# Transposing the later sequences on VectorE in 32x32 squares, with DMA moving the squares, in a linear-attention and FFN kernel

## The chip, the cores and the metric

The kernel runs on one core of a Trainium2 chip. It is one launch, all in fp32, and the time is that of the device in microseconds (us), the median of several runs. The names used below: PE is the matrix engine (TensorE), PEld its weight load, DVE is VectorE, ACT is ScalarE, POOL is GpSimd, and SP is the engine whose queue issues nearly all DMA transfers.

## The reference

The input is x, 8 sequences of 512 tokens with 512 features. The reference, cut to what matters:

```python
xn = layernorm(x)                                   # over the features
q, k, v = (xn @ W.T + b for W, b in ...)
phi = lambda t: elu(t) + 1
ctx = phi(q) * cumsum(phi(k) * v, axis=tokens) * 32 ** -0.5
s = ctx @ Wo.T + bo                                 # linear attention
h = fwht(xn * SU_ug)                                # Walsh-Hadamard transform
h = silu((h @ W_gate.T) * scale_g) * ((h @ W_up.T) * scale_u)
f = (fwht(h * SU_dp) @ W_down.T) * scale_d          # hidden size 2048
out = x + s * silu(f)
```

The matrix products want the features of xn on the partitions, so each normalized sequence has to be transposed, from tokens x features to features x tokens, before anything else can be done with it.

## The kernel before

**Passes.** The 8 sequences are handled in four passes (p = 0 to 3) of two sequences each. The two sequences of a pass are put side by side as one 1024-token operand, and each product with a weight matrix is done by a seven-product scheme in the manner of Strassen and Winograd: the operand and the weights are cut into 2x2 blocks and encoded by additions and subtractions into seven factors, and seven products P1, P2, P7, P3, P4, P5, P6 take the place of eight. The gate and up products of passes 1 to 3 apply the scheme twice, an outer and an inner one. The Hadamard transforms are folded into the weights during pass 0.

**The token operand xo.** `xo` holds the encoded tokens: seven outer factors, and for each of them seven inner factors. Of the outer ones, P1 and P2 come from the even sequence of a pair and P7 and P3 from the odd one; P5, P6, P7 and P4 are then subtractions of these. The function `transposed` (L165 to L183) makes them: for each 128 tokens of a sequence, PE transposes four 128x128 squares into a PSUM bank of tag "t" (L170), ACT copies them into `xo` (L174 for the even sequence, L177 for the odd one), and DVE makes the differences straight from PSUM (L178 to L180), and P4 at the end (L183). `inner_tokens` (L185 to L189) makes the inner P5, P6 and P4 with three subtractions of 128x1792, and `inner_t3` the inner P7 later.

**One pass.** The main loop (L986 to L1033) does, for each pass: attention (`attention`), then four hidden units u = 0 to 3 (gate, up, silu and product; `gate` and `up` in pass 0, `hidden_unit` in passes 1 to 3), with the output projection of the attention (`project_out`) inside u = 0. The product with W_down is done in halves: `down(p, 0)` after u = 1, whose result is stored to DRAM (`put_by`), and `down(p, 1)` after u = 3, which adds the first half back in, applies silu, multiplies with s and adds x. At u = 3 (pass 0) or u = 2 (passes 1 and 2), `next_x` loads the next two sequences and normalizes them (`load_x`, `layernorm`); `transposed` for both comes right before `down(p, 1)`, and then the first half d, the attention's s and the residual y are fetched.

**Products of the down projection.** `token_groups` (L404 to L501) does the seven products for two row groups g = 0, 1, each in its own PSUM bank of tag "px" (three banks) and "pz" (two banks), while tag "py" has one bank for both. The order is P1 and P7 of both groups, then P2 of g 0, P6 of g 0, P2 of g 1, P6 of g 1, and then P5, P3 and P4 of both groups. `read` (L425 to L432) takes a px bank into sa, sb or sc with an addition of the first half (L431), and `output` (L434 to L437) adds py or pz to that (L435). In the very last `down`, P4 of group 1 is done in two chunks of 128 rows, each with its own addition (L480) and its own end of the work (`gated_last`, L765 to L770).

**What sets the order.** A product is not issued where it is written, but put on an agenda by `at(place, ...)`, where a place is about one product later than the one before; `advance` works the agenda off. Work inside `background()` gets a lower priority. The planner of the framework then fixes the order of the instructions on each engine when the kernel is built, by priorities and its own estimates, so the order on each engine is the same in every run. Weights come through a queue three deep (`ask(3)`) into a pool of four tiles. The pools that matter here: `xin` has one tile (the sequence just loaded), `t8` six tiles of 1 MB, `snap` six, `xop` one.

Of the kernel before, what the change touches and what calls it, by code (L numbers as in the profile page):

```python
# [21 lines left out]
def kernel(  # L22
# [27 lines left out]
    nc = tc.nc  # L50
# [54 lines left out]
    def load_x(b, t=None, parts=1):  # L105
        if t is None:
            t = xin.tile([P, 3, 7, P], F32, tag="x", name=f"x_{b}")
            t = t.rearrange("p c s e -> p (c s e)")[:, : NT * D].rearrange("p (n d) -> p n d", n=NT)
        n = NT // parts
        for i in range(0, NT, n):  # L110
            nc.sync.dma_start(
                t[:, i : i + n], x[b, i * P : (i + n) * P, :].rearrange("(n p) d -> p n d", p=P)
            )
        return t
# [19 lines left out]
    def first_layernorms(xs):  # L134


        mv = small.tile([P, 2 * NT, 2], F32, tag="mv2", bufs=1, name="mv_first")
        rs = small.tile([P, 2 * NT, 2], F32, tag="rs2", bufs=1, name="rs_first")
        then = []

        def pinned(ins):
            tc.keep_in_program_order(ins)

        for i in range(2 * NT + 1):
            if i < 2 * NT:
                x, r = xs[i // NT][:, i % NT, :], rs[:, i, 0:1]
                st = small.tile([P, 6], F32, tag="st2", bufs=4, name=f"st_first_{i}")
                pinned(nc.vector.bn_stats(st, x))
                pinned(nc.vector.bn_aggr(mv[:, i, :], st))
                pinned(nc.vector.tensor_scalar(r, mv[:, i, 1:2], EPS, None, ALU.add))  # L150
                nc.scalar.activation(r, r, AF.Sqrt)
            if i:
                x, m, r = xs[(i - 1) // NT][:, (i - 1) % NT, :], mv[:, i - 1, 0:1], rs[:, i - 1, 0:1]
                n = rs[:, i - 1, 1:2]
                pinned(nc.vector.reciprocal(r, r))
                if i <= NT:
                    pinned(nc.vector.scalar_tensor_tensor(n, m, -1.0, r, ALU.mult, ALU.mult))
                    nc.scalar.activation(x, x, AF.Identity, bias=n, scale=r)
                else:
                    pinned(nc.vector.tensor_scalar(x, x, m, r, ALU.subtract, ALU.mult))  # L160

# [164 lines left out]
        advance(max([0] + [e[0] + 1 - now[0] for e in agenda]))  # L328

    def bank(tag, name, n):  # L330
        return ps.tile([P, n, L // n], F32, tag=tag, bufs={"px": 3, "py": 1, "pz": 2}[tag], name=f"{tag}_{name}")


    def group(name, ws, rhs, dst, then, bias=(None, None)):
# [69 lines left out]
    def token_groups(name, n, tok, wts, dst, add=None, early=None, done=None, last=None):  # L404

        px, py, pz = {}, {}, {}
        sums, ws = {}, {}

        def product(p, i, g, first, ks=None, cs=range(2)):
            if i not in ws:
                ws[i] = wts(i)
            for k in ks or range(n):
                t = tok(k, i)
                for c in cs:
                    nc.tensor.matmul(  # L420
                        p[:, c], t[:, (2 * g + c) * P : (2 * g + c + 1) * P], ws[i](k),
                        start=(first and k == 0 and c == 0), stop=(k == n - 1), skip_group_check=True,
                    )

        def read(what, o, a, s, g):  # L425
            if o is None:
                o = snap.tile([P, 2, 2 * P], F32, tag="s", name=f"{what}_{name}_{g}")
            if add is None:
                nc.scalar.copy(o, px[g])
            else:  # L430
                nc.vector.tensor_tensor(o, px[g], add(a, s, g), ALU.add)  # L431
            return o  # L432

        def output(o, p, a, s, g):  # L434
            nc.vector.tensor_tensor(dst(a, s, g), o, p, ALU.add)  # L435
            if done:
                done(a, s, g)  # L437

        def p1(g, ks=None):
            if g not in px:  # L440
                px[g] = bank("px", f"{name}_{g}", 2)
            product(px[g], P1, g, True, ks)
            if ks is None or n - 1 in ks:
                sums["a", g] = read("sa", None, 0, 0, g)

        def p7(g, ks=None):
            if g not in pz:
                pz[g] = bank("pz", f"{name}_{g}", 2)
            product(pz[g], P7, g, True, ks)

        def p2(g):
            py[g] = bank("py", f"{name}_{g}", 2)
            product(py[g], P2, g, True)
            output(sums["a", g], py[g], 0, 0, g)

        def p6(g):
            product(px[g], P6, g, False)
            sums["b", g] = read("sb", None, 1, 0, g)

        def p5(g):  # L460
            product(px[g], P5, g, False)
            s = read("sc", None, 1, 1, g)
            output(s, pz[g], 1, 1, g)

        def p3(g):
            product(px[g], P3, g, False)
            read("", dst(0, 1, g), 0, 1, g)
            if done:
                done(0, 1, g)

        def p4(g):
            if g == 0 or not last:
                product(pz[g], P4, g, False)
                output(sums["b", g], pz[g], 1, 0, g)
                return
            for c in range(2):
                product(pz[g], P4, g, False, cs=(c,))
                s = slice(c, c + 1)
                o = dst(1, 0, g)[:, s]
                nc.vector.tensor_tensor(o, sums["b", g][:, s], pz[g][:, s], ALU.add)  # L480
                last(c)

        steps = [(p, g) for p in (p1, p7) for g in range(2)]
        place = 0
        if early:
            a, b = range(early), range(early, n)
            for p, g in steps:
                at(place, lambda p=p, g=g: p(g, a))
                place += early
            place = max([place] + [e[0] - now[0] for e in agenda])  # L490
            for p, g in steps:
                at(place, lambda p=p, g=g: p(g, b))
                place += n - early
            steps = []
        steps += [(p2, 0), (p6, 0), (p2, 1), (p6, 1)]
        steps += [(p, g) for p in (p5, p3, p4) for g in range(2)]
        for p, g in steps:
            at(place, lambda p=p, g=g: p(g))
            place += n
        advance(place)  # L500
        between()  # L501
# [127 lines left out]
    def fetch(name):  # L629
        t = t8.tile([P, NT, D], F32, tag="t", name=name)  # L630
        nc.sync.dma_start(t.rearrange("p n d -> p (n d)"), kept[name])
        return t
# [353 lines left out]
    for p in range(B // 2):  # L986
        if p:
            with background():
                inner_tokens(xo)
        co = attention(p, xo, get_w)  # L990
        if p:
            inner_t3(xo, (P1, P5, P6, P2, P7))
            at(9, lambda: inner_t3(xo, (P3, P4)))
        more = p + 1 < B // 2
        hos = []

        def next_x():
            xs = [load_x(2 * p + 2), load_x(2 * p + 3)]
            for s in range(2):
                layernorm(2 * p + 2 + s, xs[s])  # L1000
            return xs

        for u in range(NU):
            if p == 0:
                gs = [gate(p, u, xo, get_w)]
                gs.append(gate(p, u + NU, xo, get_w))
                if u == 0:
                    project_out(p, co, get_w)
                ho = hop.tile([P, 2, 7, L], F32, tag="h", name=f"ho_{p}_{u}")
                for m in range(2):  # L1010
                    up(p, u + m * NU, gs[m], xo, ho[:, m], get_w)
            else:
                ho = hop.tile([P, 2, 7, L], F32, tag="h", name=f"ho_{p}_{u}")
                hidden_unit(p, u, xo, ho, get_w, u % 2 == 1)
                if u == 0:
                    project_out(p, co, get_w)
            hos.append(ho)
            if more and u == (2 if p else 3):
                xs = next_x()
            if u == 1:  # L1020
                down(p, 0, hos, get_w)
                hos = []
        if more:
            xo = xop.tile([P, 7, 7, H], F32, tag="xo", name=f"xo_{p + 1}")
            for s in range(2):
                transposed(2 * p + 2 + s, xs[s], xo)
        ds, ss = [], []
        for s in range(2):
            ds.append(fetch(f"d_{p}_{s}"))
            ss.append(fetch(f"s_{p}_{s}"))  # L1030
        ys = [load_y(p, s) for s in range(2)]
        down(p, 1, hos, get_w, ds, ss, ys)
        drain()  # L1033

# [49 lines left out]
```

## Time and profile before

| | |
|---|---|
| median of 3 runs | 1601.99 us (1600.81 to 1603.28) |
| profiled execution | 1604.14 us |
| its span, first to last instruction | 1602.3 us |
| mean granted PE clock | 0.991 of full speed |
| PE busy | 1553.3 us (97%) |
| DVE busy | 944.5 us (59%) |
| ACT busy | 429.0 us (27%) |
| POOL busy | 505.7 us (32%) |
| DMA | 254.29 MB in 148,043 packets, 7,296 of them under 512 bytes |

How to read it: busy time is the time in which an engine had an instruction in work, as a share of the span. The profile also has a chain of work that ended last, followed back from the last instruction, which says on which engine the time lay; groups of instructions by line, engine and shape, with their number, busy time, mean duration and the idle time before them with what ended it; a list of what each engine waited for ("PE px_dn L420 <- DVE sb_dn L431: 1.7, 2, 0.9" says that PE at L420 waited for the DVE instruction of L431 1.7 us in all, 2 times, 0.9 at most); a timeline of single instructions; and windows, which give the busy time of each engine in a stretch of time and the clock that PE was granted in it.

### The profile page before, as it was taken

What the parts mean: (1) busy time and instruction counts of PE and PEld (TensorE: products, weight loads), DVE (VectorE), ACT (ScalarE), POOL (GpSimd) and SP (SyncE); (2) the same over time, 40 slices, a digit from 0 to 9 for tenths busy, and PEclk for the clock granted to TensorE, in tenths of its full rate; (3) what the DMA queues carried; (4) which work ended last, traced back from release to release, by engine and by line L of the source; (5) the groups of instructions that cost most, each with busy time, mean ns of one, the idle gap of its engine ahead of it and who ended that gap; (6) DMA issues with size and microseconds to landing.
All of it is one profiled execution on the core that took longest, in us unless ns stands there. A gap on an engine that the chain in (4) does not pass through costs nothing.

```text
span 1602.3 us, 15711 instructions
## 1 busy us (share of the span) xinstructions
PE 1553.3 (97%) x5936; PEld 1118.1 (70%) x5936; DVE 944.5 (59%) x1346; ACT 429.0 (27%) x688; POOL 505.7 (32%) x286
## 2 busy tenths in 40 slices
PE   7889889999999999999999999999999999999998
PEld 3336435854485488888886478888887468888887
DVE  6868666268564574715675475634675466542673
ACT  4342332132324431111223531111221441111211
POOL 4531342104331335302622236201622137120731
PEclk9999989999999999999999999999999999999999
DMA  8234559287753244335564232535574224425472
GB/s 273 81 118 122 180 156 298 79 280 223 254 214 121 71 137 152 124 116 189 177 247 145 92 111 100 190 91 188 161 263 157 69 92 138 174 86 190 141 257 88
DMA packets 148043, 254.29 MB, mean 159 GB/s; under 512 B 7296, under 2 KB 109696, under 8 KB 143872
## 3 DMA queue, kind: packets, MB, share of 16 engines
q1 hardware_dynamic: 147824, 253.26, 47.9%
q8 instruction: 47, 0.77, 0.2%
q14 instruction: 28, 0.23, 0.0%
q10 hardware_dynamic: 144, 0.03, 0.0%
HBM read 183.53 MB, written 69.73 MB: 158 GB/s over the span
## 4 chain that ended last, share of the span: by engine, by line
PE 78%; DVE 9%; DMA 4%; POOL 3%; issue 3%; ACT 2%; SPq 0%; POOLq 0%; ACTq 0%; DVEq 0%
PE px_gu L512 18%; PE pz_gu L512 9%; PE px_dn L420 8%; PE py_gu L512 5%; PE pz_dn L420 4%; PE px_o L420 3%; PE px_v L344 3%; PE px_k L344 3%; PE px_q L344 3%; PE px_gate L344 2%; PE px_up L344 2%; PE py_dn L420 2%; POOL s L757 2%; PE pz_o L420 2%; PE pz_k L344 2%
## 5 line engine op out<-in xcount | busy, mean ns | idle before, releaser
L512 PE MATMUL px_gu<-xo,w_gu 128*128 128x256 f32 x1344 | 320.6, 379 | 0.0
L512 PEld LDWEIGHTS px_gu<-xo,w_gu 128*128 128x128 f32 x1344 | 254.6, 190 | 40.0 <-issue 3.6
L420 PE MATMUL px_dn<-w_down,ho 128*128 128x256 f32 x1024 | 230.1, 379 | 2.4 <-DVE sb_dn L431 1.7
L420 PEld LDWEIGHTS px_dn<-w_down,ho 128*128 128x128 f32 x1024 | 193.6, 190 | 31.7 <-DVE sb_dn L431 2.7
L512 PE MATMUL pz_gu<-xo,w_gu 128*128 128x256 f32 x672 | 173.1, 380 | 0.0
L712 POOL TENSOR_TENSOR u<-u,v 128x1024 f32<-128x1024 f32 x24 | 56.1, 2362 | 354.2 <-DVE u L550 354.2
L512 PEld LDWEIGHTS pz_gu<-xo,w_gu 128*128 128x128 f32 x672 | 127.0, 190 | 19.2 <-DVE a L554 0.9
L420 PE MATMUL pz_dn<-w_down,ho 128*128 128x256 f32 x512 | 116.9, 380 | 3.7 <-POOL ho L200 1.9
L420 PEld LDWEIGHTS pz_dn<-w_down,ho 128*128 128x128 f32 x512 | 96.3, 190 | 19.7 <-POOL ho L200 2.7
L757 POOL TENSOR_TENSOR s<-s,d 128x512 f32<-128x512 f32 x30 | 43.1, 1437 | 166.1 <-ACT d L756 166.1
L512 PE MATMUL py_gu<-xo,w_gu 128*128 128x256 f32 x336 | 86.2, 379 | 0.0
L600 POOL TENSOR_TENSOR v<-v,k 128x1024 f32<-128x1024 f32 x16 | 39.4, 2463 | 138.0 <-ACT v L575 109.8
L674 POOL TENSOR_TENSOR ho<-g,u 128x512 f32<-128x512 f32 x8 | 17.8, 2226 | 187.1 <-DVE u L360 187.1
L512 PEld LDWEIGHTS py_gu<-xo,w_gu 128*128 128x128 f32 x336 | 63.8, 190 | 8.7
L344 PE MATMUL px_k<-xo,w_k 128*128 128x512 f32 x128 | 63.1, 615 | 3.5 <-ACT sa_k L356 3.5
L344 PE MATMUL px_up<-xo,w_up 128*128 128x512 f32 x128 | 61.5, 609 | 3.5 <-DVE w_up L206 3.5
L716 POOL TENSOR_TENSOR v<-v,r 128x1024 f32<-128x1024 f32 x24 | 56.2, 2360 | 25.6 <-DVE r L550 25.6
L344 PE MATMUL px_v<-xo,w_v 128*128 128x512 f32 x128 | 60.4, 593 | 2.0 <-ACT sc_v L356 2.0
L344 PE MATMUL px_q<-xo,w_q 128*128 128x512 f32 x128 | 60.2, 593 | 0.0
L602 DVE TENSOR_TENSOR_SCAN k<-ones,v 128x512 f32<-128x512 f32 x32 | 39.4, 1271 | 34.9 <-POOL v L600 34.9
L344 PE MATMUL px_gate<-xo,w_gate 128*128 128x512 f32 x128 | 59.6, 593 | 0.0
L420 PE MATMUL px_o<-w_o,co 128*128 128x256 f32 x256 | 58.3, 381 | 0.0
(254 smaller groups left out, 2472.1 us busy)
## 6 DMA issues: line engine op xcount, KB each, us to landing
w_gu<-d_gu SPq DMA_DIRECT2D x84, 896.0 KB, 4.5
w_down<-d_down SPq DMA_DIRECT2D x56, 512.0 KB, 3.6
d_s<-o SPq DMA_DIRECT2D x8, 1024.0 KB, 4.9
d_d<-dn SPq DMA_DIRECT2D x8, 1024.0 KB, 7.4
d<-d_d SPq DMA_DIRECT2D x8, 1024.0 KB, 6.2
s<-d_s SPq DMA_DIRECT2D x8, 1024.0 KB, 7.4
y<-in_x_dram SPq DMA_DIRECT2D x8, 1024.0 KB, 7.8
out_dram<-y SPq DMA_DIRECT2D x15, 512.0 KB, 3.1
```

The source lines that it names most:

```text
L344: nc.tensor.matmul(p.rearrange("p a t -> p (a t)") if len(r.shape) == 2 else p, ws[k][:, i, :], r, start=(first and k == 0), stop=(k == n ...
L420: nc.tensor.matmul(p[:, c], t[:, (2 * g + c) * P : (2 * g + c + 1) * P], ws[i](k), start=(first and k == 0 and c == 0), stop=(k == n - 1), ...
L512: nc.tensor.matmul(p[:, lane], w[:, lane, i, :], x[:, i, :], start=(first and lane == 0), stop=True, skip_group_check=True,)
L600: nc.gpsimd.tensor_tensor(v[:, h], v[:, h], k[:, h], ALU.mult)
L602: nc.vector.tensor_tensor_scan(k[:, h, s], ones.to_broadcast([P, L]), v[:, h, s], 0.0, ALU.mult, ALU.add)
L674: nc.gpsimd.tensor_tensor(ho[:, P1], g[:, 0, 0], r[:, 0, 0], ALU.mult)
L712: nc.gpsimd.tensor_tensor(r[:, m], ru1[:, m], rv[:, m], ALU.add)
L716: nc.gpsimd.tensor_tensor(rv[:, m], rv[:, m], rr[:, m], ALU.add)
L757: (nc.vector if final and (a, s) == (1, 0) else nc.gpsimd).tensor_tensor(r, r, d, ALU.mult)
```

## The change

The first two sequences are transposed by PE as before. For the other six:

- `normalized(b)` loads and normalizes one sequence and stores it back to a DRAM buffer of its own. It is called, with background priority, in the hidden units u = 0 and u = 1 of each pass but the last, one sequence in each; `next_x` is gone.
- `squares(b)` loads it again, in four DMA transfers, such that each run of 32 features of one token goes to the partition that the transposed layout wants for this token's place in its group of 32. One transfer fills 32 partitions with 64 x 32 elements each, in runs of 128 bytes. The tile z that it fills is the `xin` tile for an even sequence and a `t8` tile for an odd one.
- `turned` transposes the 32x32 squares in place with `nc.vector.transpose` on DVE, one instruction for 128 partitions x 512 elements, four for a sequence, straight from z into `xo`.
- `next_tokens` takes the place of the two calls of `transposed`: loads, the transposes, and the four outer differences as subtractions of 128x1024. The second half of the odd sequence with two of the differences is put on the agenda at place 5, and P4 at place 10.
- `xo` is no longer allocated anew in each pass: the same tile is written again.
- d is fetched for both sequences at once, s at place 7 of the agenda and y at place 15.
- In the last `down`, P7 and P4 of group 1 use two banks, one for each chunk of rows: the pz bank and one of tag "t".

```diff
+    def normalized(b):
+        xt = load_x(b)
+        layernorm(b, xt)
+        d = dram.tile([L, D], F32, tag=f"d_x_{b}", name=f"d_x_{b}")
+        nc.sync.dma_start(d.rearrange("(n p) d -> p n d", p=P), xt)
+        kept[f"x_{b}"] = d
+
+    def squares(b):
+        if b % 2:
+            z = t8.tile([P, KD, L], F32, tag="t", name=f"z_{b}")
+        else:
+            z = xin.tile([P, 3, 7, P], F32, tag="x", name=f"z_{b}")
+            z = z.rearrange("p c s e -> p (c s e)")[:, : KD * L].rearrange("p (c t) -> p c t", c=KD)
+        d = kept[f"x_{b}"].rearrange("(i t) (c j f) -> j t c i f", t=32, j=4, f=32)
+        for j in range(4):
+            nc.sync.dma_start(z[32 * j : 32 * j + 32].rearrange("p c (i f) -> p c i f", f=32), d[j])
+        return z
+
+    def turned(place, z, h, xo):
+        for j in range(2):
+            nc.vector.transpose(
+                xo[:, place, j : j + 3 : 2, :], z[:, 2 * h + j]
+            )
+
+    def next_tokens(b, xo):
+        o = xo[:, :, 0:4]
+        za, z = squares(b), squares(b + 1)
+        turned(P1, za, 0, xo)
+        turned(P2, za, 1, xo)
+        turned(P7, z, 0, xo)
+        nc.vector.tensor_tensor(o[:, P5], o[:, P7], o[:, P1], ALU.subtract)
+
+        def rest():
+            turned(P3, z, 1, xo)
+            nc.vector.tensor_tensor(o[:, P6], o[:, P3], o[:, P5], ALU.subtract)
+            nc.vector.tensor_tensor(o[:, P7], o[:, P3], o[:, P7], ALU.subtract)
+
+        def last():
+            nc.vector.tensor_tensor(o[:, P4], o[:, P2], o[:, P6], ALU.subtract)
+
+        at(5, rest)
+        at(10, last)
...
         def p7(g, ks=None):
...
-            product(pz[g], P7, g, True, ks)
+            if g == 1 and last:
+                if "t" not in pz:
+                    pz["t"] = bank("t", name, 2)
+                product(pz[g], P7, g, True, ks, cs=(0,))
+                product(pz["t"], P7, g, True, ks, cs=(1,))
+            else:
+                product(pz[g], P7, g, True, ks)
...
         def p5(g):
             product(px[g], P5, g, False)
             s = read("sc", None, 1, 1, g)
-            output(s, pz[g], 1, 1, g)
+            if g == 0 or not last:
+                output(s, pz[g], 1, 1, g)
+                return
+            for c in range(2):
+                nc.vector.tensor_tensor(dst(1, 1, g)[:, c], s[:, c], pz[g if c == 0 else "t"][:, c], ALU.add)
+            done(1, 1, g)
...
             for c in range(2):
-                product(pz[g], P4, g, False, cs=(c,))
-                s = slice(c, c + 1)
-                o = dst(1, 0, g)[:, s]
-                nc.vector.tensor_tensor(o, sums["b", g][:, s], pz[g][:, s], ALU.add)
+                p = pz[g if c == 0 else "t"]
+                product(p, P4, g, False, cs=(c,))
+                nc.vector.tensor_tensor(dst(1, 0, g)[:, c], sums["b", g][:, c], p[:, c], ALU.add)
                 last(c)
...
-            if more and u == (2 if p else 3):
-                xs = next_x()
+            if more and u < 2:
+                with background():
+                    normalized(2 * p + 2 + u)
             if u == 1:
                 down(p, 0, hos, get_w)
                 hos = []
         if more:
-            xo = xop.tile([P, 7, 7, H], F32, tag="xo", name=f"xo_{p + 1}")
-            for s in range(2):
-                transposed(2 * p + 2 + s, xs[s], xo)
-        ds, ss = [], []
-        for s in range(2):
-            ds.append(fetch(f"d_{p}_{s}"))
-            ss.append(fetch(f"s_{p}_{s}"))
-        ys = [load_y(p, s) for s in range(2)]
+            next_tokens(2 * p + 2, xo)
+        ds = [fetch(f"d_{p}_{s}") for s in range(2)]
+        ss, ys = [], []
+        at(7, lambda: ss.extend([fetch(f"s_{p}_{s}") for s in range(2)]))
+        at(15, lambda: ys.extend([load_y(p, s) for s in range(2)]))
         down(p, 1, hos, get_w, ds, ss, ys)
```

More of the change, by code (lines that the diff above doesn't have):

```diff
@@ L330, in bank @@
     def bank(tag, name, n):
-        return ps.tile([P, n, L // n], F32, tag=tag, bufs={"px": 3, "py": 1, "pz": 2}[tag], name=f"{tag}_{name}")
+        return ps.tile([P, n, L // n], F32, tag=tag, bufs={"px": 3, "py": 1, "pz": 2, "t": 2}[tag], name=f"{tag}_{name}")
     def group(name, ws, rhs, dst, then, bias=(None, None)):
@@ L421, in product @@
                         p[:, c], t[:, (2 * g + c) * P : (2 * g + c + 1) * P], ws[i](k),
-                        start=(first and k == 0 and c == 0), stop=(k == n - 1), skip_group_check=True,
+                        start=(first and k == 0 and c == cs[0]), stop=(k == n - 1), skip_group_check=True,
                     )
@@ L995 @@
         hos = []
-        def next_x():
-            xs = [load_x(2 * p + 2), load_x(2 * p + 3)]
-            for s in range(2):
-                layernorm(2 * p + 2 + s, xs[s])
-            return xs
         for u in range(NU):
@@ L1023 @@
         if more:
-            xo = xop.tile([P, 7, 7, H], F32, tag="xo", name=f"xo_{p + 1}")
-            for s in range(2):
-                transposed(2 * p + 2 + s, xs[s], xo)
-        ds, ss = [], []
-        for s in range(2):
-            ds.append(fetch(f"d_{p}_{s}"))
-            ss.append(fetch(f"s_{p}_{s}"))
-        ys = [load_y(p, s) for s in range(2)]
+            next_tokens(2 * p + 2, xo)
[3 more added lines that the diff above has]
+        at(15, lambda: ys.extend([load_y(p, s) for s in range(2)]))
         down(p, 1, hos, get_w, ds, ss, ys)
```

## The prediction

> **What bounds the kernel now.** I read the share of engines and the chain first, then the groups by shape, the waits of TensorE (PE), the timeline at the pass boundaries, and windows for the granted clock.
>
> ```profile
> PE 1553.3 (97%) x5936; PEld 1118.1 (70%) x5936; DVE 944.5 (59%) x1346; ACT 429.0 (27%) x688; POOL 505.7 (32%) x286
> ...
> PE 78%; DVE 9%; DMA 4%; POOL 3%; issue 3%; ACT 2%; SPq 0%; POOLq 0%; ACTq 0%; DVEq 0%
> ...
> L170 PE MATMUL pt<-ident,x 128*128 128x128 f32 x128 | 19.8, 299 | 8.9 <-ACT x L158 7.4 <-ACT xo L174 0.8 <-DVE x L129 0.6
> ...
> PE px_dn L420 <- DVE sb_dn L431: 1.7, 2, 0.9
> ...
> PE pz_dn L420 <- DVE d L480: 1.8, 1, 1.8
> ```
>
> PE is the bound, and outside the first 240 us it hardly waits: the second half of the list of its waits (two of its lines above) comes to about 10 us. So two things decide: PE time that vanishes, and waits of PE that appear. The boundary from pass 1 to pass 2:
>
> ```profile
> 806.32 0.87 PE pt L170 x8
> ...
> 829.38 0.89 PE pt L170 x8
> ```
> ```profile
> 817.20 1.23 DVE L703 TENSOR_TENSOR ho<-u 128x1024 f32<-128x1024 f32 x1 [1.24 <-ACT u L702]
> ...
> 818.46 1.23 DVE L697 TENSOR_TENSOR ho<-ho 128x1024 f32<-128x1024 f32 x1
> ...
> 830.17 0.68 DVE L435 TENSOR_TENSOR d<-sa_dn,py_dn 128x512 f32<-128x512 f32 x1
> ...
> 833.99 3.62 PE L420 MATMUL py_dn<-w_down,ho 128*128 128x256 f32 x16
> ...
> 836.59 1.22 DVE L183 TENSOR_TENSOR xo<-xo 128x1024 f32<-128x1024 f32 x1
> ...
> 838.92 2.02 DVE L187 TENSOR_TENSOR xo<-xo 128x1792 f32<-128x1792 f32 x1
> ```
>
> The first fence is the chain: eight transposes cost the path 0.87 to 0.89 us, 0.109 us each (the group's mean of 299 ns overlaps its neighbours). The second is the timeline: VectorE (DVE) reads the only py bank at 830.17, PE refills it at 833.99 (P2 of row group 1), and the subtractions L183, L187 to L189 come after that read.
>
> **What goes.** Six of eight sequences lose 16 transposes each: 96 x 0.109 = **10.4 us of PE**. ACT loses 24 copies (L174, L177) and DVE 36 subtractions of 128x256, both beside PE.
>
> **What comes on DVE.** 24 square transposes of 128x512. The trace has no such row. From below: the layernorm scale (L129) steps 0.46 us per 128x512; from above, twice a 128x512 add, 1.2 us. I take T = 0.65, nearest to the 128x512 add of equal shape (0.61 back to back, 0.68 alone). [...]
>
> **Where they stand.** The planner fixes each engine's order at build; the order of the changed program on DVE at each boundary is: last encode of ho, three transposes of the odd sequence, the P5 subtraction, the fourth transpose, sa of group 0, the P6, P7, P4 subtractions, sa of group 1, the three inner subtractions (L187 to L189 before), and **only then the read of py** (L435 before). In the kernel before that read stood ahead of L183 and L187 to L189. Queued behind it on DVE are sb of both groups and the residual adds; waiting for it on PE is P2 of group 1, since py has one bank.
>
> Pass 1, on the old time scale. DVE is free for the transposes at about 818.3: the last L697 above ends at 819.7, less 0.96 of ACT copies that stood between two silu halves and some 0.4 of PE transposes. Then 4T, four 128x1024 (1.15 + 3 x 1.14), two sa reads (0.6 each), three 128x1792 (1.93 each) and the py read (0.6): 818.3 + 12.2 + 4 x 0.65 = **833.1**. PE, without 32 transposes (3.5 us) and the 0.9 us of waits between them, is there at 829.6. It stalls 3.5 us and starts P2 of group 1 0.9 us earlier than before. The wait for sb_dn (0.86, second line of waits above) falls away: the pass nets -1.75 us out of 3.5 removed. Pass 2 has the same order: -1.75. The even sequence's four transposes lie in the blocks of the last hidden unit, each 6.04 us with about 5 of DVE work; +0.65 fits.
>
> Pass 0: both sequences are turned at the boundary, 8T in a row from 444.8: 444.8 + 12.2 + 5.2 = 462.2. PE, held by the POOL wait (pz_dn<-ho L200) until 449.9, arrives at 458.6 and stalls 3.5 us. Before, P2 of group 1 began at 460.45 and 16 transposes (1.75) followed, together 462.2: **net 0**.
>
> **The clock.** A PE pause is dearer than its length:
>
> ```profile
> 495.90:499.30 3.40, 3.36 (x5) 1.35 (x6) 1.30 (x3) 0.00 (x0) 1.13 (x1) 0.55 0.77 305
> ...
> 867.30:870.70 3.40, 3.40 (x8) 1.63 (x9) 1.29 (x2) 0.69 (x1) 0.71 (x1) 1.00 1.00 335
> ```
>
> These are windows; the third number from the right is the granted clock. After an idle of 2.3 us it was 0.55 for 3.4 us, after one of 1.0 us full; after the 3.5 us wait at 197 us it was 0.50 for 5.5 us. By the counts of products such a drop costs 1.6 to 2.8 us; I take 2.0. [...]
>
> **The transfers.** Each sequence is stored to DRAM normalized (1 MB, 2048-byte packets, 84 ns each in the record of packets) and loaded again in four transfers of 2048 runs of 128 bytes: 49,152 packets against 148,043 in all. Packet time in the trace is 18 ns at 256 bytes and 27 at 512, on a line to about 13 at 128; over 16 engines that is 1.7 us per transfer, 14 for eight. Upper: the trace never moved more than about 680 packets/us, 3.0 us per transfer. [...] Due times: at pass 0 they issue around 428 and are wanted at 445 to 447: 428 + 14 + 2 fits, by the upper bound they land at 452 to 454 (+4 to +7 us). In passes 1 and 2 the even sequence is loaded in the attention phase, the odd one between 789 and 811 for 818: covered by about 7 us even so.
>
> **Smaller terms.** Layernorm of the next sequences moves into the first two hidden units: 5.8 us of DVE each, during waits that it has there, with one Sqrt and two table loads (1.28 each) on ACT. In pass 0 ACT evicts folded weights then, so +0.3 (0 to 3); later hidden. SP issues 30 more transfers at 0.3 to 0.5 us, with seconds in hand between weights; the stores may move a weight load by 2 to 3 us, less than the three-deep prefetch. s and y are fetched later (places 7 and 15 of the agenda), still ahead of their adds. The last product in two banks removes the 1.79 us wait of the last chunk for the L480 read, but DVE's own last add ends 0.8 us behind: -0.8 (-0.7 to -1.7).
>
> **Sum** against the profiled 1604.14 us (span 1602.3 and 1.8 around it): pass 0 +2.0; pass 1 -1.75 + 2.0 = +0.25; pass 2 +0.25; moved layernorm +0.3; tail -0.8: **+2.0**. On the median of the runs, 1602.0, that gives **1604**. [...]
>
> **Rivals.**
> 1. *The removed PE time stays removed* (faster). DVE gets through sooner, or the stalls stay under what the clock notices: -10.4 - 0.8 + up to 4 of stall = 1591 to 1598. For it: PE is 97% busy, and T of 0.46 alone takes 0.8 us off the stalls of 3.5. Against: the count 12.2 + 4T of back-to-back DVE work ahead of the py read. Without the clock drops alone, 1598.
> 2. *The small transfers bind at pass 0* (slower). [...] It decides from 2.3 us per transfer on. For it: no row under 256 bytes; against: the line of packet times.
> [...]
>
> **Chances.** Forecast 0.42 (own range 1599 to 1609: 0.05 faster, 0.23 same, 0.14 slower), rival 1 0.25, rival 2 0.20, rival 3 0.10, something else 0.03. Faster 0.30, same 0.24, slower 0.46, where the bound of 0.2% (3.2 us) is about what a measurement can tell. Leaving out 0.1 at each end gives 1593 to 1618.
>
> **What would show it.** PE's waits list a new px/py_dn wait for the py read (or for xo behind it) of about 3.5 us at three boundaries, with a clock near 0.5 for 3.4 us behind each; the transposes have a row with T; PE's busy time falls by some 6 to 10. Wrong if: no such wait (rival 1); DVE idle ahead of the first transpose, released by z's DMA (rival 2); T near 1.2 (rival 3); or PE waits in the first 300 us, from the moved layernorm, which I put at 0.3.

## The result, and the profile after

The changed kernel takes 1603.78 us (median of 14 runs, 1601.08 to 1608.16), the kernel before 1602.82 us (14 runs, 1599.97 to 1607.42). The ratio is 1.0005, with a 95% interval of 0.9995 to 1.0015: no difference that can be measured. The span of the profiled execution is 1601.9 us, its mean PE clock 0.988.

That is not because nothing happened. First the share of engines, from the page:

```profile
PE 1543.6 (96%) x5840; PEld 1112.4 (69%) x5840; DVE 957.7 (60%) x1344; ACT 417.9 (26%) x664; POOL 501.8 (31%) x286
```

PE does 96 instructions less and is busy 9.7 us less, and DVE is busy 13 us more. PE's saved time was replaced by a wait. The list of PE's waits (us in all, times, longest) and the group of the transposes (busy us, mean ns):

```profile
PE py_dn L469 <- DVE d L484: 11.1, 3, 4.0
...
PE px_k L393 <- ACT sa_k L405: 2.1, 2, 1.1
```
```profile
L187 DVE STREAM_TRANSPOSE xo<-z 128x512 f32<-128x512 f32 x24 | 15.8, 690 | 2.9 <-PE px_gu L571 2.9
```

The first line did not exist before: three waits of PE for the read of the py bank, 11.1 us together. The two waits for sb_dn (1.7 us) and the one for d at the end (1.8 us) are gone from the list. The timeline at the boundary from pass 1 to pass 2, which answers to the one shown of before (start, duration, engine, line, operation, and in brackets the idle time before it):

```profile
817.78 1.89 DVE L187 STREAM_TRANSPOSE xo<-z 128x512 f32<-128x512 f32 x3
...
825.55 3.62 PE L469 MATMUL px_dn<-w_down,ho 128*128 128x256 f32 x16
825.89 2.01 DVE L236 TENSOR_TENSOR xo<-xo 128x1792 f32<-128x1792 f32 x1
827.94 2.02 DVE L237 TENSOR_TENSOR xo<-xo 128x1792 f32<-128x1792 f32 x1
830.00 2.02 DVE L238 TENSOR_TENSOR xo<-xo 128x1792 f32<-128x1792 f32 x1
831.94 0.68 DVE L484 TENSOR_TENSOR d<-sa_dn,py_dn 128x512 f32<-128x512 f32 x1
832.54 0.68 DVE L480 TENSOR_TENSOR sb_dn<-px_dn,d 128x512 f32<-128x512 f32 x1
832.68 5.38 PE L469 MATMUL py_dn<-w_down,ho 128*128 128x256 f32 x16 [3.51 <-DVE d L484]
```

The three inner subtractions (L236 to L238 now) run before the read of py (L484), PE idles 3.51 us, and the 16 products that follow take 5.38 us where 16 took 3.62 at 825.55. The windows behind the three waits show why (third number from the right: the granted clock):

```profile
461.60:468.20 6.60, 6.53 (x17) 5.30 (x18) 1.31 (x3) 0.63 (x1) 1.26 (x1) 0.56 0.01 2
832.60:838.00 5.40, 5.32 (x17) 4.47 (x18) 1.31 (x3) 0.63 (x1) 1.26 (x1) 0.68 0.01 3
1203.00:1209.00 6.00, 6.00 (x17) 4.82 (x17) 0.83 (x2) 0.26 (x1) 1.26 (x1) 0.57 0.00 0
```

From P2 of group 1 to the first product of the next pass takes 27.9 us at full clock without waits (28.76 us in pass 1 of the kernel before, less its wait of 0.86). In the changed kernel it takes 30.57, 29.39 and 30.45 us: the slow clock costs 2.7, 1.5 and 2.6 us, **6.7 us** on top of the 11.1.

Where time goes between the two profiled executions, by the start of the first product of k in each pass. Each column is one execution; in these two the changed kernel ends 0.6 us earlier, where the medians put it 1.0 us later, so a line of about a microsecond can belong to the execution rather than to the change.

| first k product of | before | after | lead of before | change over the pass | forecast |
|---|---|---|---|---|---|
| pass 1 | 490.07 | 492.24 | +2.17 | +2.2 | +2.3 |
| pass 2 | 862.75 | 862.07 | -0.68 | -2.9 | +0.25 |
| pass 3 | 1232.45 | 1233.05 | +0.60 | +1.3 | +0.25 |
| last addition | 1599.34 | 1598.73 | -0.61 | -1.2 | -0.8 |

### The profile page after: what moved, and what is told of

Read it like the earlier page. It is cut to its first block, busy times and chain, and to the rows that moved or that the text cites. A ratio compares the mean times of both kernels' runs of the same rounds, so it can differ in the third digit from the quotient of the medians.

```text
span 1601.9 us, 15535 instructions
## 1 busy us (share of the span) xinstructions
PE 1543.6 (96%) x5840; PEld 1112.4 (69%) x5840; DVE 957.7 (60%) x1344; ACT 417.9 (26%) x664; POOL 501.8 (31%) x286
## 5 line engine op out<-in xcount | busy, mean ns | idle before, releaser
L469 PE MATMUL pz_dn<-w_down,ho 128*128 128x256 f32 x496 | 112.7, 380 | 2.7 <-POOL ho L249 2.7
L816 POOL TENSOR_TENSOR s<-s,d 128x512 f32<-128x512 f32 x30 | 38.4, 1280 | 173.3 <-ACT d L815 173.3
L469 PE MATMUL py_dn<-w_down,ho 128*128 128x256 f32 x256 | 65.4, 414 | 11.1 <-DVE d L484 11.1
L469 PEld LDWEIGHTS py_dn<-w_down,ho 128*128 128x128 f32 x256 | 53.7, 211 | 20.7 <-DVE d L484 12.3
L815 ACT ACTIVATE d<-d 128x512 f32<-128x512 f32 x31 | 19.5, 630 | 178.0 <-DVE d L484 123.2
```

Source lines behind the costliest of these rows:

```text
L469: nc.tensor.matmul(p[:, c], t[:, (2 * g + c) * P : (2 * g + c + 1) * P], ws[i](k), start=(first and k == 0 and c == cs[0]), stop=(k == n - ...
L815: nc.scalar.activation(d, d, AF.Silu)
L816: (nc.vector if final and (a, s) == (1, 0) else nc.gpsimd).tensor_tensor(r, r, d, ALU.mult)
```

## The experiments

Each time stands beside runs of the kernel before on the same chip, and the ratio is to those. The changes are to the changed kernel where nothing else is said.

**The inner subtractions held back.** The three subtractions get a later place on the agenda, in the attention of the next pass, and are pinned to the order of the program, so that the planner cannot move them forward again.

```diff
     def inner_tokens(xo):
-        nc.vector.tensor_tensor(xo[:, :, P5], xo[:, :, P7], xo[:, :, P1], ALU.subtract)
+        tc.keep_in_program_order(nc.vector.tensor_tensor(xo[:, :, P5], xo[:, :, P7], xo[:, :, P1], ALU.subtract))
... (the same for P6 and P4)
         if p:
-            with background():
-                inner_tokens(xo)
+            at(8, lambda: inner_tokens(xo))
```

> The changed kernel with the three inner subtractions (128x1792, 6.1 us together) held back on VectorE until the attention of the next pass; nothing else moves. Theory (they stand in front of the read of the only py bank, and PE's pause then halves its clock): the read ends 6.1 us earlier, before PE is there, so the waits for it (11.1 us in three) and the slow stretches behind them (2.7 + 1.5 + 2.6 = 6.7 us) go: about 1586 us, ratio to the kernel before 0.989. Rival (the work only moves: the subtractions now stand in front of the attention's reads of k, and PE waits there): 6 us come back per pass, ratio 0.999 to 1.001.

Measured: 1585.17 us, ratio 0.9892 (0.9870 to 0.9915). The wait for L484 is gone from PE's list. The timeline at the same boundary as above:

```profile
818.98 0.68 DVE L480 TENSOR_TENSOR sa_dn<-px_dn,d 128x512 f32<-128x512 f32 x1
819.22 3.62 PE L469 MATMUL px_dn<-w_down,ho 128*128 128x256 f32 x16
819.58 0.68 DVE L484 TENSOR_TENSOR d<-sa_dn,py_dn 128x512 f32<-128x512 f32 x1
822.68 3.62 PE L469 MATMUL py_dn<-w_down,ho 128*128 128x256 f32 x16
822.88 0.69 DVE L480 TENSOR_TENSOR sb_dn<-px_dn,d 128x512 f32<-128x512 f32 x1 [2.62 <-PE px_dn L469]
```

The read of py starts 3.1 us before PE begins P2 of group 1, and those products follow without a gap in 3.62 us. Six us of subtractions in front of one read cost some 18 us of the kernel; moved into the attention phase they cost nothing that can be seen. The rival, a new wait in the attention, did not come.

**A second bank for py.** The same wait, taken away at the other end, with DVE's order untouched.

```diff
         def p2(g):
-            py[g] = bank("py", f"{name}_{g}", 2)
+            py[g] = bank("t" if g and add and early and not last else "py", f"{name}_{g}", 2)
```

> The changed kernel with P2 of row group 1 in an idle bank of tag t in the three down projections that wait; VectorE's order stays as it is. Theory (one bank for py is what ties PE to VectorE's queue there): PE does not wait for the read of group 0 any more, the next thing that it needs from that queue (sb of group 0, before P5) is due 6.9 us later: about 1586 us, ratio 0.989, as with the subtractions held back. Rival (PE is tied to VectorE's queue by more than this bank, so the wait moves to px): ratio 0.995 to 1.001.

Measured: 1586.70 us, ratio 0.9894 (0.9872 to 0.9916). All that PE still waits for from DVE at the boundaries is 0.3 us, once, for sb_dn. So it is this one bank through which DVE's queue reached PE, and not the queue's length as such.

**The wait filled.** To part the pause from the clock, PE was given useless work inside the pause.

```diff
         def p2(g):
+            if g and add and early and not last:
+                product(bank("t", f"fill_{name}", 2), P2, g, True, range(3))
             py[g] = bank("py", f"{name}_{g}", 2)
```

> The changed kernel with 12 further products of 128x256 (2.6 us of PE, into an idle bank that nobody reads) put on PE in front of P2 of row group 1, inside the wait. VectorE's order and the length of the wait's end stay. Theory (the pause halves the clock): the idle left is 0.9 to 1.4 us, the clock stays full, and the 6.7 us of slow products go although PE has more to do: about 1597 us, ratio 0.996. Rival (the clock's fall costs nothing, since what follows waits for VectorE anyway): ratio 1.000 to 1.001.

Measured: 1596.37 us, ratio 0.9958 (0.9943 to 0.9972). PE does more and the kernel is faster. Its timeline at the boundary:

```profile
829.87 2.75 PE L469 MATMUL t_fill_dn<-w_down,ho 128*128 128x256 f32 x12
...
832.81 0.68 DVE L484 TENSOR_TENSOR d<-sa_dn,py_dn 128x512 f32<-128x512 f32 x1
...
833.54 3.72 PE L469 MATMUL py_dn<-w_down,ho 128*128 128x256 f32 x16 [0.93 <-DVE d L484]
```

PE still cannot start before the read ends, but the products behind it take 3.72 us instead of 5.38. The ratio lies 0.47% under that of the changed kernel, 7.5 us, which is the 6.7 us of slow products within the intervals.

**Less filling.**

```diff
-                product(bank("t", f"fill_{name}", 2), P2, g, True, range(3))
+                product(bank("t", f"fill_{name}", 2), P2, g, True, range(1))
```

> The changed kernel with 4 further products (0.86 us of PE) in front of P2 of row group 1: the idle left is 2.6, 2.6 and 3.2 us. If an idle of 2.3 us halves the clock each time, as one did in the kernel before, all three stretches behind stay slow: 1603 to 1604 us. If it depends on more than the length (an idle of 3.0 us in pass 0 of the changed kernel halved nothing), some of them are fast: 1598 to 1602.

Measured: 1601.45 us, ratio 0.9997 (0.9986 to 1.0008). The time alone decides nothing here, the timeline does:

```profile
464.31 5.26 PE L469 MATMUL py_dn<-w_down,ho 128*128 128x256 f32 x16 [3.17 <-DVE d L484]
...
833.80 3.72 PE L469 MATMUL py_dn<-w_down,ho 128*128 128x256 f32 x16 [2.67 <-DVE d L484]
...
1201.73 5.20 PE L469 MATMUL py_dn<-w_down,ho 128*128 128x256 f32 x16 [2.66 <-DVE d L484]
```

Idle times of 2.67 and 2.66 us, in the same place of two passes: over the 3.4 us behind the first the granted clock was 1.00, behind the second 0.55. So here the length alone did not decide; the last section has more such pairs.

**The transposes twice.**

```diff
         for j in range(2):
-            nc.vector.transpose(
-                xo[:, place, j : j + 3 : 2, :], z[:, 2 * h + j]
-            )
+            for _ in range(2):
+                nc.vector.transpose(
+                    xo[:, place, j : j + 3 : 2, :], z[:, 2 * h + j]
+                )
```

> The changed kernel with every square transpose done twice (24 more of 0.61 us back to back). Theory (eight of them in pass 0 and four in each of passes 1 and 2 lie on the path to the py read): 4.9 + 2.4 + 2.4 = 9.8 us more, about 1613 us, ratio 1.0065. Rival (they lie beside other work): ratio 1.000 to 1.002.

Measured: 1607.58 us, ratio 1.0036 (1.0026 to 1.0045), so some 5 us over the changed kernel by the ratios and not 9.8. The transposes took 0.69 us each, as before. But the planner, with more work at hand, ordered DVE anew. The timeline:

```profile
833.39 2.02 DVE L238 TENSOR_TENSOR xo<-xo 128x1792 f32<-128x1792 f32 x1
835.33 0.68 DVE L485 TENSOR_TENSOR d<-sa_dn,py_dn 128x512 f32<-128x512 f32 x1
835.93 2.02 DVE L239 TENSOR_TENSOR xo<-xo 128x1792 f32<-128x1792 f32 x1
```

The read of py (L485 here) now goes ahead of the last inner subtraction, and that gives 2.05 us back at each boundary: 9.8 - 3 x 2.05 = 3.7 us. PE's waits there are 5.6, 4.0 and 4.0 us against 4.0, 3.5 and 3.5, so 2.4 us longer in all. They grew although one subtraction had left the path, so the transposes lie on it; what one of them costs cannot be read from this run, because the order changed with it.

**The loads of z in long runs.** The same bytes, but whole rows of 8 KB for a partition.

```diff
-        d = kept[f"x_{b}"].rearrange("(i t) (c j f) -> j t c i f", t=32, j=4, f=32)
+        d = kept[f"x_{b}"].rearrange("(q n) d -> q (n d)", n=4)
         for j in range(4):
-            nc.sync.dma_start(z[32 * j : 32 * j + 32].rearrange("p c (i f) -> p c i f", f=32), d[j])
+            nc.sync.dma_start(z[32 * j : 32 * j + 32].rearrange("p c t -> p (c t)"), d[32 * j : 32 * j + 32])
```

> The changed kernel with the four loads of z taking whole rows of 8 KB per partition in place of runs of 128 bytes: the same bytes to the same tile, in the wrong places, so the squares hold other tokens. Theory (the small transfers are over before VectorE is ready for them: in pass 0 they move from 425.8 to 440.1 us, the first transpose is at 443.5): no change against the changed kernel, 1603 to 1604 us, ratio to the kernel before 1.0005. Rival (they take issue time of SP, 1.5 us each, and DMA time from the weights): 2 us or more faster than the changed kernel, ratio under 0.9993.

Measured: 1590.50 us, ratio 0.9932 (0.9916 to 0.9947). This is far from what the theory expected, and its rival seemed to win. The timeline of the boundary says otherwise:

```profile
823.11 2.01 DVE L236 TENSOR_TENSOR xo<-xo 128x1792 f32<-128x1792 f32 x1
...
825.04 0.68 DVE L484 TENSOR_TENSOR d<-sa_dn,py_dn 128x512 f32<-128x512 f32 x1
825.64 2.02 DVE L237 TENSOR_TENSOR xo<-xo 128x1792 f32<-128x1792 f32 x1
```

The order on DVE is another one here too: the transposes and the outer subtractions had moved up between the last blocks of the hidden unit, and the py read ahead of two of the three inner subtractions. PE waits for it once, 1.1 us. Whether the transfers themselves cost anything was open, so the same loads were put into the kernel with the early read, where such a reordering has nothing to win.

> The kernel with the inner subtractions held back, and the loads of z in whole rows of 8 KB in place of runs of 128 bytes (the squares hold other tokens). The long loads alone took the changed kernel to 1590.5 us, but the planner had moved VectorE's transposes forward with them, so the order and not the transfers may be the cause. Theory (the transfers cost nothing, what the long loads won was the earlier py read): with the read early anyway there is nothing left to win, 1584 to 1587 us, as with short runs (1585.2). Rival (the short runs cost DMA or SP time by themselves): 4 to 12 us faster, 1573 to 1581.

Measured: 1588.04 us, ratio 0.9901 (0.9885 to 0.9918), against 0.9892 with short runs: nothing gained. The intervals leave room for about 4 us, so the traces have to decide. Passes 1 and 2 together take 728.65 us with long runs and 728.99 us with short ones, so the small transfers cost nothing there that shows. Pass 0 is 3.3 us longer with long runs: DVE's order differs again, and PE waits 2.4 us for POOL in place of 1.4, with the clock at 0.62 behind it. A small cost of the transfers in pass 0 could hide behind that, and is not excluded by this run. What the long runs won in the changed kernel was another order from the planner.

**The price of a transpose on PE.** In the kernel with the inner subtractions held back, 96 transposes of the identity put back on PE.

```diff
         for j in range(2):
+            pt = ps.tile([P, KD, P], F32, tag="t", name=f"pt_{place}_{h}_{j}")
+            for c in range(KD):
+                nc.tensor.transpose(pt[:, c, :], ident, ident)
             nc.vector.transpose(
```

> The kernel with the inner subtractions held back, and 96 transposes of 128x128 put back on PE (of the identity, into a bank that nobody reads), in the first boundary; VectorE's order is the same. Theory (a removed transpose is worth its 0.109 us of PE wherever no wait of PE covers it): 10.4 us more, less up to 1.4 that the wait for POOL there can cover: 1594 to 1596 us, ratio to the kernel before 0.995 to 0.996. Rival (the gain of 17 us comes from the waits and the clock alone, the transposes were hidden): 1585 to 1587.

Measured: 1596.40 us, ratio 0.9958 (0.9943 to 0.9972) against 0.9892: 0.66%, 10.6 us. The planner put all 96 into the first boundary, between 432.7 and 462.2 us, and there the traces show the cost: the first product of k in pass 1 starts at 496.82 us against 485.90 without them, and pass 1 takes 364.41 us against 364.40. So the transposes put back here, which no wait of PE covered, cost their whole 0.109 us each (10.6 / 96 = 0.110). That the 96 were worth as much in their old places, 32 at each boundary, rests on the chain of the kernel before (0.87 to 0.89 us for eight) and not on this run.

**The tail in one bank.** In the kernel with the inner subtractions held back, P7 and P4 of group 1 in one pz bank again.

```diff
-                product(pz[g], P7, g, True, ks, cs=(0,))
-                product(pz["t"], P7, g, True, ks, cs=(1,))
...
+            product(pz[g], P7, g, True, ks)
... (the addition after P5 in one piece again)
-                p = pz[g if c == 0 else "t"]
+                p = pz[g]
```

> The kernel with the inner subtractions held back, and the last product in one bank as in the kernel before. Theory (the second bank took away a wait of 1.8 us on PE, but VectorE ends the chain only 0.6 to 0.8 us sooner): 0.6 to 0.8 us slower than with two banks, some 1586; from the last product of row group 0 to the last addition 0.6 us longer in the trace. Rival (the second bank is worth its whole wait): 1.8 us.

Measured: 1587.65 us, ratio 0.9911 (0.9892 to 0.9929). The interval is too wide for a difference of this size. In the timelines, from the start of the last 24 products of pz to the start of the last addition it is 1582.96 - 1572.44 = 10.5 us with one bank and 1580.57 - 1570.76 = 9.8 with two: 0.7 us, and not the 1.8 of PE's wait.

**The next sequences normalized later.** In the kernel with the inner subtractions held back, in pass 0 at u = 1 and 2.

```diff
-            if more and u < 2:
+            if more and (p == 0) <= u < 2 + (p == 0):
                 with background():
-                    normalized(2 * p + 2 + u)
+                    normalized(2 * p + 2 + u - (p == 0))
```

> The kernel with the inner subtractions held back, and in pass 0 the two normalizations in the hidden units u = 1 and 2 in place of 0 and 1. Theory (the moved layernorm costs pass 0 about 0.3 us): within 1 us of the same kernel with u = 0 and 1, 1584 to 1586 us. Rival (VectorE and ACT are full in the folding of weights, and the layernorm there adds to PE's wait for g, 3.5 us before and 3.6 to 5.2 since): 1.5 to 3 us faster, 1582 to 1584.

Measured: 1593.44 us, ratio 0.9954 (0.9938 to 0.9970). Neither theory nor rival: slower than with u = 0 and 1, by 10 us by the ratios and by 8.0 us in the traces, all of it in pass 0. PE's waits have two lines that are new:

```profile
PE px_gate L393 <- ACT sc_gate L403: 4.7, 1, 4.7
...
PE pz_dn L469 <- DVE u L409: 3.0, 1, 3.0
```

The timeline has the cause of the second: DVE is free for the layernorm from 277.64 us (283.64 less the wait of 6.00), 0.9 us before its load is even issued.

```profile
278.53 0.39 SPq L111 DMA_DIRECT2D x<-in_x_dram  x1
...
283.64 1.29 DVE L122 BATCH_NORM_STATS2 st<-x 128x6 f32<-128x512 f32 x2 [6.00 <-DMA x<-in_x_dram]
284.85 0.67 DVE L409 TENSOR_TENSOR u<-sb_up,pz_up 128x512 f32<-128x512 f32 x1
...
285.57 4.16 PE L469 MATMUL pz_dn<-w_down,ho 128*128 128x256 f32 x12 [3.05 <-DVE u L409]
```

DVE waits 6.0 us for x, L409 stands behind it, PE waits for L409, and its 12 products then take 4.16 us where 12 take 2.75. The first line is the same by way of ACT, whose Sqrt (L126) waits for the statistics ahead of the copy of sc_gate. Once more it is a wait at the head of a fixed queue.

## Why the prediction was right

The forecast was 1604 us, +2.0 us on the kernel before, in the range of 1593 to 1618; measured are 1603.78 and a ratio of 1.0005, whose interval of -0.8 to +2.4 us holds the forecast. By its own steps:

- **What goes.** 10.4 us of PE: 96 transposes put back, though all at one boundary, cost 10.6 us.
- **T.** 0.65 us taken; measured 0.69 us on the mean, and about 0.60 from one start to the next (three in 1.89 us). The row of the addition of equal shape was the right one; twice such an addition, 1.2 us, which was taken as the limit from above, is 1.7 times the measured mean. No run shows a T near 1.2, the value that the third rival stands for.
- **The place of the py read.** Right: 831.94 us for its start and 3.51 us of PE idle in pass 1, where 833.1 for its end and 3.5 were worked out; 4.03 and 3.53 in passes 0 and 2, where 3.5 was. Two independent removals (the subtractions, the bank) each brought the changed kernel down by 1.1%, some 18 us.
- **The clock.** 2.0 us for each of three boundaries, 6.0; measured 6.7, in parts of 2.7, 1.5 and 2.6, and filling the pause returned it. That all three were hit was likely but not certain: waits of 3.61 and 3.67 us elsewhere in the runs were followed by full clock (last section).
- **Pass 0.** The forecast of 2.0 for the boundary and 0.3 for the moved layernorm gave +2.3; the traces give +2.2, but not from these parts. By the first product px_gate after 230 us the changed kernel is 2.6 us ahead (234.10 against 236.70), and that is luck: up to 228 us both kernels have the same order on PE, DVE and ACT, and two waits of PE, of 3.05 us at 148 us and of 3.0 to 3.5 us at 200 us, left the clock whole in the changed kernel (1.00 over the 3.4 us behind each) and not in the kernel before (0.65 and 0.50). In nine later runs whose order is the changed kernel's up to there, this product starts anywhere from 234.9 to 238.2 us. The stretch with the moved layernorm then takes 1.4 us longer than before (from this product to the product that waits for POOL, 288.71 - 234.10 = 54.6 against 289.95 - 236.70 = 53.3), 0.7 of it a new wait for ACT's copy of sc_up; 0.3 was too little. Over the boundary the changed kernel loses 3.4: 4.0 of idle and 2.7 of slow clock, less 3.5 for 32 transposes, is +3.2. Of the 1.4 that the forecast was short there, 0.5 is the stall and 0.7 the clock.
- **Passes 1 and 2.** +0.25 each; measured -2.9 and +1.3. The first has a term that was not in the sum, PE's wait for sa_k at the start of pass 1, here before and after:

```profile
495.94 3.52 PE L344 MATMUL px_k<-xo,w_k 128*128 128x512 f32 x4 [2.27 <-ACT sa_k L356]
...
496.88 1.98 PE L393 MATMUL px_k<-xo,w_k 128*128 128x512 f32 x4 [1.05 <-ACT sa_k L405]
```

  It was 2.27 us in the kernel before, with a slow clock behind it (0.55 over 3.4 us), and 1.05 in the changed kernel, with none (1.00). From the first k product to the first of pz_k it took 499.25 - 490.07 = 9.2 us before and 498.70 - 492.24 = 6.5 after, 2.7 us less, 1.2 of it the wait and 1.5 the clock. Without that pass 1 is at -0.1. Whether the longer wait is the rule in the kernel before or belonged to this execution, its one trace cannot tell. Pass 2 lost 2.6 to the clock where 2.0 was taken, the rest of its 1.0 was not traced further.
- **The tail.** -0.8 forecast; the second bank gave about 0.7 in the traces. The -1.2 of the table has 0.5 more from the attention at the start of pass 3, which was not traced further.

So the mechanism is the forecast one, and each of its large terms is near. That the sum came out closer than its terms is luck: 2.6 us before the first layernorm and 2.7 us at the start of pass 1 fell in its favour unforeseen, and against it the three boundaries cost about 2 us and the layernorm 1.1 us more than forecast.

The rivals: "the removed PE time stays removed" is what the kernel with the subtractions held back does, and 1585 us is below the 1591 to 1598 put on it, mainly since waits of before do not come back either: for sb_dn (1.7 us), for w_down (0.7), and the 2.7 us at the start of pass 1. "The small transfers bind" fell: the last of eight in pass 0 was issued at 435.3 us and landed at most 5.1 us later, 3 us ahead of the first transpose at 443.5. The third, a T near 1.2 us, fell with the measured 0.69. That the range reached to 1618 is the weight of these two slower rivals; no run shows what either would have cost.

Not tried: giving the planner other costs for the transfers, which might have led it to the good order without a pin.

## What to carry to other kernels

Work taken from the bounding engine is only won if what replaces it does not stand in front of something that this engine waits for: list, for each added instruction, what is behind it in its engine's fixed queue, and through which buffer the bounding engine is tied to that. A pause of PE as long as those that a slow clock followed here (2.27 us and more) should be counted with that clock, which cost 1.5 to 2.7 us at the three boundaries; if the pause cannot go, even useless products in it can pay (7.5 us here). And a term that hangs on such a pause can fall either way from one execution to the next, so two single traces that differ by 2 us need not show the change. And where a planner writes the order, an experiment that changes a cost changes the order too: compare the orders before believing the time.

## What the runs showed of the hardware that was not expected

- **Behind pauses of PE of 2.27 to 3.67 us the clock fell or it did not, and the length did not say which.** PE's wait for g at about 148 us is 3.05 to 3.06 us long in all twelve traces, and up to there all twelve kernels have the same order on PE, DVE and ACT. In five the products behind it were slow, in seven they ran at full clock (0.65 in the kernel before, 1.00 in the changed one). The kernel before and the changed one:

```profile
147.10 2.85 PE L420 MATMUL pz_o<-w_o,co 128*128 128x256 f32 x8 [3.05 <-DVE g L360]
...
148.06 2.00 PE L469 MATMUL pz_o<-w_o,co 128*128 128x256 f32 x8 [3.05 <-DVE g L409]
```

  Taking in all twelve traces each wait of PE of 0.8 us or more after the first 20 us, with the granted clock of the 3.4 us behind it: none of 60 waits up to 2.26 us was followed by a slow clock, 25 of 44 from 2.27 to 3.67 us were (0.50 to 0.71), and so were all 35 from 3.73 us up. Waits of 2.27, 2.31 and 2.66 us were hit (0.55 behind the first and the last), while the changed kernel's 3.05 us above was not (1.00). What decides between waits of equal length was not shown.
- **Runs of 128 bytes kept to the line of larger packets.** In the changed kernel's record of packets the 49,152 of 128 bytes took 13 ns each (256 bytes took 18, 512 took 27), and the eight loads of pass 0, 16,384 packets, were moved within about 14 us, as estimated. They did hold up their queue: SP spent 1.44 us (median) on each issue of these eight, which came in a row, and 0.57 us on one that stood alone, where most other transfers took 0.3 to 0.5 us.
